# A four-layer graph network on one core: one product of the batch-norm shift in layer 0, half of layer 3's merged weights formed at the layer's end, pair sums added behind the next block

## The chip, the core and the metric

The kernel runs on one core of a Trainium2 chip. The core has five engines with instruction streams of their own: TensorE (PE, matrix products into PSUM), VectorE (DVE), ScalarE (ACT), GpSimd (POOL, here used for issuing transfers) and SyncE (SP, transfers only). Each engine takes its instructions in one fixed order and waits at an instruction until what it needs is there. The metric is the device time of one execution in microseconds; lower is better. Before the change it is 3288.74 us, the median of three runs (3287.61 to 3291.08).

## What is computed

Four graph layers on 2708 nodes with 512 features and a dense 0/1 adjacency matrix; after each layer comes `x = layernorm(x + layer(x))`. The change lies in layer 0, and touches weights of layer 3:

```python
# layer 0, X = x, n = 2708, H = 4 heads of D = 128; both patterns are adj
Xw = einsum('hnd,hde->hne', Xh, W)
f1 = einsum('hnd,hd->hn', Xw, V[:, 0, :, 0])
f2 = einsum('hnd,hd->hn', Xw, V[:, 1, :, 0])
sig = sigmoid(f1[:, :, None] + f2[:, None, :])
att = softmax over j of (adj * sig) where adj != 0, else 0
Xc  = concat over heads of att @ Xw
Xn  = batchnorm(Xc, enc_bn_gamma, enc_bn_beta)
emb = batchnorm(elu(Xn @ enc_mlp_W.T + enc_mlp_b) + Xn, ...)
Y   = elu(concat over heads of (att @ emb_h) @ W_h.T)
out = batchnorm(elu(Y @ dec_mlp_W.T + dec_mlp_b) + Y, ...)
# layer 1: A @ (x @ W + b) / column degree;  layer 2: softmax(e) with e = h @ h.T, h = x @ edge_w
# layer 3: softmax((x @ Wq + bq) @ (x @ Wk + bk).T / sqrt(512) + 2 adj) @ (x @ Wv + bv)
```

In layer 3 the kernel uses the merged matrix Wq @ Wk.T, of 512 x 512, in place of the two projections.

## The kernel before

Features are held transposed (four tiles of 128 features on the partitions, nodes along the free axis) or as rows (22 blocks of 128 nodes; the last has 20). Layer 0 makes two attention passes, the first over `xw` (values X W), the second over `emb`. Each runs over two halves of the target nodes (`hf`, 1354 columns) and, in each half, two pairs of heads (`p`); each such part goes over the 22 source blocks in a fixed order, `ORDER`. One block in the first pass:

- the adjacency block `a` comes from DRAM. With p = 0, DVE turns its zeros into a large negative number (L385 into `z`, L386 into `a`), and POOL writes it to `adj_d` for later parts. `z` has the tag "z", which has one buffer;
- ACT computes tanh for both heads into `t` (L396), DVE multiplies by the mask (L404), ACT takes the exponential in place (L405). Tiles `t` have the tag "t", with four buffers;
- PE multiplies the block's values with `t` into six PSUM banks `po` (L471, six products of 450 or 452 columns);
- PE adds up `t` over the rows into `psm` for the softmax's denominators (L494, eight small products). With p = 1, the blocks at places 4 to 19 are taken in pairs: DVE adds the odd block to the even one (L488), and PE sums once.

After 22 blocks `finish` copies `po` out (for the first pass `keep`, L580); the denominators go through DRAM, and the scaling and the batch-norm statistics (L608, L609) come during the next part.

The batch norm ahead of the encoder is folded into its weights: `enc_w` is scaled by `scale1` (L683 to L688), and the bias is the layer's bias plus the product of W with the norm's beta (in `keep`, after half 0 and p = 1, L583 to L586), minus the product of the scaled W with the mean (L732 to L742, within the encoder's first chunk). `small_product` takes four products of 1 x 512 (L546), a copy of the row on DVE (L549) and four products of 1 x 1 that turn the row into a column (L551). Its row in `keep` has the tag "z".

Between the passes PE transposes Wq and Wk (L668) into `wqT` and `wkT`, which lie in rows of `emb` that aren't filled yet, and forms the merged weights from them in four groups of four products (L696), which ACT scales and copies (L703) and POOL writes to `mqk_d` (L705). Then comes the query bias (`ps_u`), and the encoder (L724) in six chunks, whose result is transposed into `emb` (L756, L757).

At the end of layer 0 (`decode`, in the part that is final) PE runs the decoder's products (L859) chunk by chunk; `r_dec` takes buffers of the tag "t". The last chunk is followed by elu, statistics and the third batch norm on DVE and ACT. Layer 1 opens pools of its own over the memory of layer 0's: `hid_hi` and `hid_lo`, `raw`, `b1_sb`, `w1_sb`. Its first writes are a memset of a part of `hid_hi` and the copy `w1_sb` on DVE (L966, L976), both queued behind the norm's shift (`ready`), and the load of `b1_sb` (L102) on SP. It then scales the chunks (L983 on ACT), adds x (L990 on DVE), transposes and projects them (L996, L128 on PE).

A framework places all waits and fixes the order of each engine ahead of the run: by readiness in a plan of its own, and by program order among those that are ready. `issue_after(ins)` puts the instructions of its block behind `ins` on the same engine. Tiles with one tag share a given number of buffers.

## Time and profile before

| | us |
|---|---|
| median of three runs | 3288.74 |
| the profiled execution | 3290.97 |
| its span (first to last instruction) | 3289.2 |
| first attention pass, first product to last sum | 44.9 to 573.9 |
| merged weights to the last product of the encoder | 586.2 to 694.0 |
| second attention pass | 694.4 to 1145.0 |
| decoder's last product ends | 1201.6 |
| layer 1's first transposition | 1209.1 |

How to read the profile: PE, PEld (weight loads of PE), DVE, ACT, POOL and SP are the engines, SPq the queue of SP. Line numbers (L471) are those of the kernel before. In a timeline a line has the start, the time in us, the engine, the line, the operation, the tile written and the tile read, shapes and a count of instructions that were merged; in brackets stands how long the engine had been idle before, and what ended it. An fp32 product shows as two records, so "x12" of L471 are six products. The chain of waits is followed back from the last instruction, each time to what released it.

### The profile page before, as it was taken

How to read it: one execution, taken by the hardware profiler on the slowest of the kernel's cores; microseconds unless marked ns; L12 is line 12 of the kernel's file. 1: busy time of each engine (PE TensorE's matmuls, PEld its weight loads, DVE VectorE, ACT ScalarE, POOL GpSimd, SP SyncE). 2: the span in 40 equal slices, each digit the busy share in tenths (PEclk: the TensorE clock that was granted, in tenths of full speed). 3: DMA queues.
4: the chain of work that ended last, by engine and by line, in shares of the span. 5: the costliest groups of instructions: out<-in, count | busy, mean ns of one | idle time of the engine just before them, and what ended most of it. 6: DMA issues, size and time to landing. Idle time of an engine off the chain costs nothing.

```text
span 3289.2 us, 30359 instructions
## 1 busy us (share of the span) xinstructions
PE 3221.7 (98%) x10922; PEld 1722.4 (52%) x10922; DVE 1944.6 (59%) x3144; ACT 1348.5 (41%) x1512; POOL 129.7 (4%) x211
## 2 busy tenths in 40 slices
PE   8998999999999999999999999999999999999999
PEld 5443444454444445885555555554455555555554
DVE  7877977767687596445136666777252452543433
ACT  6887887557877753001133434443020120210211
POOL 1100100000000000000011000000000000000000
PEclk9999999999999999999999999999999999999999
DMA  8855863335555322550034444554211111111100
GB/s 283 305 187 171 302 233 124 106 102 183 185 179 172 134 81 67 144 145 21 0 102 133 122 124 136 148 159 125 68 49 33 44 31 43 40 34 43 36 24 20
DMA packets 172550, 381.45 MB, mean 116 GB/s; under 512 B 20938, under 2 KB 115094, under 8 KB 167982
## 3 DMA queue, kind: packets, MB, share of 16 engines
q1 hardware_dynamic: 156926, 308.16, 30.9%
q0 software_dynamic: 15472, 71.33, 5.8%
q8 instruction: 86, 1.41, 0.2%
q14 instruction: 66, 0.54, 0.1%
HBM read 307.22 MB, written 71.67 MB: 115 GB/s over the span
## 4 chain that ended last, share of the span: by engine, by line
PE 88%; DVE 5%; ACT 2%; DMA 2%; issue 1%; SPq 0%; DVEq 0%; ACTq 0%
PE po L1324 23%; PE po L471 19%; PE ps_s L1203 18%; PE ps_nb L1056 6%; PE ps_wide L1105 4%; PE psm L494 3%; DVE t L404 2%; PE ps_hid L128 2%; PE ps_sup L1501 2%; PE ps_o L1432 2%; PE ps_mlp L724 2%; PE ps_dec L859 2%; DMA a<-adj_d 1%; ACT t L405 1%; ACT t L396 1%
## 5 line engine op out<-in xcount | busy, mean ns | idle before, releaser
L404 DVE SCALAR_TENSOR_TENSOR t<-t,a 128x2708 f32<-128x2708 f32 (+1 forms) x156 | 462.2, 2975 | 124.1 <-ACT t L396 120.1
L396 ACT ACTIVATE t<-f1b,f2h 128x1354 f32<-128x1354 f32 (+1 forms) x312 | 428.3, 1413 | 60.5 <-PE po L471 28.7
L471 PE MATMUL po<-t,xw 128*128 128x452 f32 (+3 forms) x1056 | 415.9, 557 | 14.6 <-ACT t L405 14.6
L405 ACT ACTIVATE t<-t 128x2708 f32<-128x2708 f32 (+1 forms) x156 | 382.6, 2455 | 112.7 <-DVE t L404 112.4
L471 PE MATMUL po<-t,emb 128*128 128x452 f32 (+3 forms) x1056 | 403.1, 550 | 12.3 <-ACT t L405 9.2
L1203 PE MATMUL ps_s<-sup,hT 128*128 128x384 f32 (+1 forms) x1176 | 407.4, 490 | 0.0
L1324 PE MATMUL po<-sup,e 128*128 128x512 f32 x882 | 407.0, 595 | 0.0
L1324 PE MATMUL po<-e,xs 128*128 128x384 f32 (+1 forms) x1176 | 406.0, 489 | 0.0
L1635 DVE SCALAR_TENSOR_TENSOR e<-a_cols,ps_s 128x384 f32<-128x384 f32 (+1 forms) x154 | 85.5, 556 | 451.1 <-PE ps_s L1203 428.2
L471 PEld LDWEIGHTS po<-t,xw 128*128 128x128 f32 (+1 forms) x1056 | 191.5, 193 | 227.4 <-issue 202.0
L1203 PEld LDWEIGHTS ps_s<-sup,hT 128*128 128x128 f32 x1176 | 221.8, 190 | 164.2 <-issue 14.2
L471 PEld LDWEIGHTS po<-t,emb 128*128 128x128 f32 (+1 forms) x1056 | 194.9, 192 | 213.5 <-issue 188.7
L1324 PEld LDWEIGHTS po<-e,xs 128*128 128x128 f32 x1176 | 222.2, 190 | 160.2 <-issue 5.8
L1324 PEld LDWEIGHTS po<-sup,e 128*128 128x128 f32 x882 | 160.4, 190 | 159.3 <-issue 137.1
L1203 PE MATMUL ps_s<-hT 128*128 128x384 f32 (+5 forms) x672 | 211.1, 461 | 0.9 <-ACT sup L1508 0.7
L1302 ACT ACTIVATE e<-e 128x384 f32<-128x384 f32 (+1 forms) x308 | 151.7, 522 | 116.0 <-DVE e L1301 113.3
L1056 PE MATMUL ps_nb<-hid_hi,at 128*128 128x512 f32 x484 | 185.4, 390 | 0.4 <-DVE at L1048 0.4
L1550 ACT ACTIVATE a_cols<-a_cols,neg_big 128x384 f32<-128x384 f32 (+1 forms) x154 | 94.7, 617 | 220.9 <-DMA a_cols<-in_adjT_dram 183.3
L1056 PE MATMUL ps_nb<-hid_lo,at 128*128 128x512 f32 x462 | 179.9, 389 | 0.0
L108 ACT ACTIVATE ln_rstd<-ln_rstd 128x1 f32<-128x1 f32 (+1 forms) x88 | 17.2, 201 | 391.7 <-DVE ln_rstd L107 391.2
L1301 DVE TENSOR_TENSOR e<-e,nmax 128x384 f32<-128x384 f32 (+1 forms) x308 | 163.1, 552 | 23.3 <-ACT nmax L1294 23.3
L1203 PEld LDWEIGHTS ps_s<-hT 128*128 128x128 f32 x672 | 123.1, 190 | 89.5 <-issue 19.4
(252 smaller groups left out, 3325.8 us busy)
## 6 DMA issues: line engine op xcount, KB each, us to landing
a<-adj_d SPq DMA_DIRECT2D x110, 677.0 KB
a_cols<-in_adjT_dram SPq DMA_DIRECT2D x378, 192.0 KB
a<-in_adjT_dram SPq DMA_DIRECT2D x42, 677.0 KB
adj_d<-a POOLq DMA_DIRECT2D x42, 677.0 KB, 5.5
raw<-in_adjT_dram SPq DMA_DIRECT2D x105, 256.0 KB
kept<-t POOLq DMA_DIRECT2D x16, 1354.0 KB, 6.8
t<-kept SPq DMA_DIRECT2D x16, 1354.0 KB
a_cols<-in_adjT_dram SPq DMA_DIRECT2D x63, 202.0 KB
```

Of the source, the lines that this page charges most:

```text
L396: nc.scalar.activation(tv[:, k, :], f1b[:n, k, :w], AF.Tanh, bias=f2h[:n, jt, h : h + 1], scale=0.5,)
L404: step = nc.vector.scalar_tensor_tensor(tv, tv, GUARD, ab, ALU.add, ALU.mult)
L405: nc.scalar.activation(tv, tv, AF.Exp, scale=0.5)
L471: nc.tensor.matmul(po[HB * k + q][:, :qw], values[r : r + n, jt, h * P : (h + 1) * P], t[r : r + n, k, q0 : q0 + qw], start=(place == 0), ...
L494: nc.tensor.matmul(sums[k][32 * r : 32 * r + 32, :SW], ones32[:m], whole[:m, k, q0 + qw - SW : q0 + qw], start=(place == 0), stop=(place = ...
L1056: nc.tensor.matmul(pos[it][:n], at, half[:, jt, :], start=(jt == 0 and k == 0), stop=(jt == NT - 1),)
L1105: nc.tensor.matmul(ps[:, :width], w(c, o), xt(c), start=(c == 0), stop=(c == C - 1),)
L1203: nc.tensor.matmul(ps[:, b * P : w], keys[:, c, j0 : j0 + P], st["q"][:, c, b * P :], start=(c == 0), stop=(c == C - 1),)
L1301: nc.vector.tensor_tensor(e, e, st["nmax"][:, :w], ALU.add)
L1302: nc.scalar.activation(e, e, AF.Exp)
L1324: nc.tensor.matmul(out, lhsT, rhs, start=(k == 0), stop=(k == NT - 1))
L1550: nc.scalar.activation(a, a, AF.Identity, bias=neg_big[: a.shape[0]], scale=1.0e30)
```

## The change

Five things are done.

1. The bias of the encoder is formed at once: `shift1` (beta minus mean times scale) is computed after the batch norm's scale, and one small product of it with the unscaled `enc_w` gives the bias. The product in `keep` and the one in the encoder's first chunk are gone. `enc_w` is scaled after the product.
2. Of the four groups of the merged weights, group 0 stays ahead of the shift's product and group 1 comes behind it. POOL writes `wkT` and half of `wqT` to DRAM (`wkT_d`, `wqT_d`), and each quarter of `mqk_d` gets its first half.
3. The other two groups are formed at the end of `decode`: `wkT_d` and `wqT_d` are loaded into two buffers of the tag "t", PE forms the groups behind the decoder's last product (`last_dec`) in two of the `po` banks, ACT copies them into the second half of one of the buffers, and POOL writes them to `mqk_d`.
4. In the paired blocks of the first pass, the add on DVE is issued behind the multiplication (L404) of the next block, and the pair's sums come just ahead of the next block's products in the program.
5. The row of the product in `keep`, with the tag "z", is gone with it.

```diff
--- before.py
+++ after.py
@@ -1,3 +1,4 @@
+from functools import partial
 from contextlib import ExitStack, nullcontext
 import concourse.bass as bass
@@ -163,6 +164,9 @@
     dram = ctx.enter_context(tc.tile_pool(name="dram", bufs=1, space=bass.MemoryType.DRAM))
     adj_d = dram.tile([N, N], F32, name="adj_d")
     mqk_d = dram.tile([C, P, C, P], F32, name="mqk_d")
+    wqT_d = dram.tile([P, C, C // 2 * P], F32, name="wqT_d")
+    wkT_d = dram.tile([P, C, F], F32, name="wkT_d")
     qscale = float(1.0 / F**0.5)
     uq = const.tile([P, C], F32, name="uq")
@@ -428,7 +432,7 @@
                     sums = None
                     if first and rest is None:
                         sums = sum_tiles()
-                    before = None
+                    before = waiting = None
                     for place, jt in enumerate(ORDER):
                         n = BLOCKS[jt][1]
@@ -464,6 +468,9 @@
                                 for q in range(HB)
                             ]
                             po = [both[q][:, k, :] for k in range(HP) for q in range(HB)]
+                        if waiting is not None:
+                            waiting(step)
+                            waiting = None
                         for k in range(HP):
                             h = HP * p + k
                             for q, (q0, qw) in enumerate(HCH[hf]):
@@ -478,26 +485,37 @@
                         if not first:
                             continue
-                        if prepare or not ALONE <= place < NT - LAST:
-                            whole, m = t, n
-                        elif place % 2 == 0:
+                        single = prepare or not ALONE <= place < NT - LAST
+                        if not single and place % 2 == 0:
                             before = t
                             continue
+                        def add_up(whole, m, more, first_one, last_one, behind=None):
+                            if more is not None:
+                                with tc.issue_after(behind.ins):
+                                    nc.vector.tensor_tensor(
+                                        whole[: more.shape[0], :, :w],
+                                        whole[: more.shape[0], :, :w],
+                                        more,
+                                        ALU.add,
+                                    )
+                            for k in range(HP):
+                                for r, (q0, qw) in enumerate(SCH[hf]):
+                                    nc.tensor.matmul(
+                                        sums[k][32 * r : 32 * r + 32, :SW],
+                                        ones32[:m],
+                                        whole[:m, k, q0 + qw - SW : q0 + qw],
+                                        start=first_one,
+                                        stop=last_one,
+                                    )
+                        if single:
+                            add_up(t, n, None, place == 0, place == NT - 1)
                         else:
-                            whole, m = before, P
-                            nc.vector.tensor_tensor(
-                                whole[:n, :, :w], whole[:n, :, :w], tv, ALU.add
-                            )
-                        for k in range(HP):
-                            for r, (q0, qw) in enumerate(SCH[hf]):
-                                nc.tensor.matmul(
-                                    sums[k][32 * r : 32 * r + 32, :SW],
-                                    ones32[:m],
-                                    whole[:m, k, q0 + qw - SW : q0 + qw],
-                                    start=(place == 0),
-                                    stop=(place == NT - 1),
-                                )
+                            waiting = partial(add_up, before, P, tv, False, False)
                     later += finish(hf, p, po, sums if first else rb) or []
             for work in later:
                 work()
@@ -580,10 +598,6 @@
                         taken[q % 2] = copy(
                             ft[:, HP * p + k, h0 + q0 : h0 + q0 + qw], po[HB * k + q][:, :qw]
                         )
-                if hf == 0 and p == 1:
-                    row = att.tile([P, HW], F32, tag="z", name="row", bufs=1)[:1, :F]
-                    ps = small_product(po[0], mlp_w[0], prm_sb[:, B_ENC, :], row)
-                    nc.vector.tensor_tensor(bias[:, 0, :], ps, prm_sb[:, MB_ENC, :], ALU.add)
                 sm = [att.tile([P, BW], F32, tag="rs", name="sm") for _ in range(HP)]
                 if not final:
                     for k in range(HP):
@@ -640,6 +654,7 @@
             attention_pass(xw, True, att, psum, keep, f1b, blocks, spread, rest, taken)
             scale1, mean1 = batch_scale(stats, G_ENC, "bn1")
+            shift1 = batch_shift(scale1, mean1, B_ENC, "bn1")
             emb = rows_tile("emb")
@@ -676,21 +691,9 @@
             tc.tile_pool(name="ps_c", bufs=1, space=PSUM) as psum,
         ):
-            (enc_w,) = mlp_w
-            for c in range(C):
-                if c % 2:
-                    nc.scalar.activation(
-                        enc_w[:, c, :], enc_w[:, c, :], AF.Copy, scale=scale1[:, c : c + 1]
-                    )
-                else:
-                    nc.vector.tensor_scalar(
-                        enc_w[:, c, :], enc_w[:, c, :], scale1[:, c : c + 1], None, ALU.mult
-                    )
-            stats = stats_tile("stats_b", NCH)
             mqk = emb[:, NT - 3 * C : NT - 2 * C, :]
-            for c in range(C):
+            def merged(c):
                 ps = psum.tile([P, F], F32, tag="misc", name="ps_m", bufs=2)
                 for o in range(C):
                     nc.tensor.matmul(
@@ -701,10 +704,38 @@
                         stop=(o == C - 1),
                     )
                 nc.scalar.activation(mqk[:, c, :], ps, AF.Copy, scale=qscale)
+            merged(0)
+            (enc_w,) = mlp_w
+            row = emb[:1, NT - 3 * C - 2 : NT - 3 * C, :]
+            pm = small_product(
+                psum.tile([P, F], F32, tag="misc", name="ps_shift", bufs=2),
+                enc_w,
+                shift1,
+                row[:, 1, :],
+            )
+            nc.vector.tensor_tensor(bias[:, 0, :], pm, prm_sb[:, MB_ENC, :], ALU.add)
+            nc.vector.tensor_scalar(bias[:, 1, :], bias[:, 0, :], 1.0, None, ALU.subtract)
+            for c in range(C):
+                if c % 2:
+                    nc.scalar.activation(
+                        enc_w[:, c, :], enc_w[:, c, :], AF.Copy, scale=scale1[:, c : c + 1]
+                    )
+                else:
+                    nc.vector.tensor_scalar(
+                        enc_w[:, c, :], enc_w[:, c, :], scale1[:, c : c + 1], None, ALU.mult
+                    )
+            stats = stats_tile("stats_b", NCH)
+            nc.gpsimd.dma_start(wkT_d, wkT)
+            nc.gpsimd.dma_start(wqT_d, wqT[:, :, half * P :])
+            merged(1)
             for o in range(C):
-                nc.gpsimd.dma_start(mqk_d[o], mqk[:, :, o * P : (o + 1) * P])
-            row = emb[:1, NT - 3 * C - 2 : NT - 3 * C, :]
+                nc.gpsimd.dma_start(
+                    mqk_d[o][:, :half, :], mqk[:, :half, o * P : (o + 1) * P]
+                )
             pu = small_product(
                 psum.tile([P, F], F32, tag="misc", name="ps_u", bufs=2),
                 wkT,
@@ -729,17 +760,6 @@
                             stop=(c == C - 1),
                         )
                     pss.append(ps)
-                    if ci == 0 and o == 0:
-                        pm = small_product(
-                            psum.tile([P, F], F32, tag="misc", name="ps_mean", bufs=2),
-                            enc_w,
-                            mean1,
-                            row[:, 1, :],
-                        )
-                        nc.vector.tensor_tensor(bias[:, 0, :], bias[:, 0, :], pm, ALU.subtract)
-                        nc.vector.tensor_scalar(
-                            bias[:, 1, :], bias[:, 0, :], 1.0, None, ALU.subtract
-                        )
                 for o in range(C):
                     dst = ft[:, o, c0 : c0 + w]
                     r = elu(
@@ -768,6 +788,7 @@
             dec_w = load_mlp(dec_wT, "dec_w")
             links = {}
             spare = []
+            last_dec = [None]
             def centre(pm):
@@ -856,7 +877,7 @@
                     q0, qw = HCH[hf][q]
                     ps = psum.tile([P, BANK], F32, tag="misc", name="ps_dec", bufs=2)
                     for c in range(C):
-                        nc.tensor.matmul(
+                        last_dec[0] = nc.tensor.matmul(
                             ps[:, :qw],
                             dec_w[:, c, o * P : (o + 1) * P],
                             t[:, c, q0 : q0 + qw],
@@ -942,6 +963,38 @@
                     if q == 0:
                         centre(po[0])
                     mlp(q, 3, st, True)
+                rest = [
+                    att.tile([P, HP, HW], F32, tag="t", name=name, bufs=4).rearrange(
+                        "p k w -> p (k w)"
+                    )
+                    for name in ("wk_again", "wq_again")
+                ]
+                wk_again = rest[0][:, : C * F].rearrange("p (c o) -> p c o", c=C)
+                wq_again, mqk = [
+                    rest[1][:, k * half * F : (k + 1) * half * F] for k in range(2)
+                ]
+                wq_again = wq_again.rearrange("p (c o) -> p c o", c=C)
+                mqk = mqk.rearrange("p (c o) -> p c o", c=half)
+                nc.sync.dma_start(wk_again, wkT_d)
+                nc.sync.dma_start(wq_again, wqT_d)
+                with tc.issue_after(last_dec[0].ins):
+                    for c in range(half):
+                        for o in range(C):
+                            nc.tensor.matmul(
+                                po[1 + c],
+                                wq_again[:, o, c * P : (c + 1) * P],
+                                wk_again[:, o, :],
+                                start=(o == 0),
+                                stop=(o == C - 1),
+                            )
+                for c in range(half):
+                    nc.scalar.activation(mqk[:, c, :], po[1 + c], AF.Copy, scale=qscale)
+                    nc.gpsimd.dma_start(
+                        mqk_d[:, :, half + c, :].rearrange("o p i -> p o i"),
+                        mqk[:, c, :].rearrange("p (o i) -> p o i", o=C),
+                    )
             attention_pass(emb, False, att, psum, decode)
         dsum = small.tile([P, NT], F32, tag="dsum", name="dsum")
```

## The prediction, made before the changed kernel was run

> **What bounds the kernel now.** I read the page first: busy times, then the chain that ended last.
>
> ```profile
> PE 3221.7 (98%) x10922; PEld 1722.4 (52%) x10922; DVE 1944.6 (59%) x3144; ACT 1348.5 (41%) x1512; POOL 129.7 (4%) x211
> PE 88%; DVE 5%; ACT 2%; DMA 2%; issue 1%; SPq 0%; DVEq 0%; ACTq 0%
> ```
>
> TensorE (PE) is busy 98% of the span and holds 88% of the chain. So time is won in two ways: PE work that moves into a gap of PE, and gaps of PE that close. All that is changed lies before 1210 us, and I looked for the gaps there in the timelines. The passes of the first attention are called (half, pair) = (0,0), (0,1), (1,0), (1,1).
>
> The largest gap is at the seam from (0,1) to (1,0). PE, then VectorE (DVE), in order of time:
>
> ```profile
> 299.32 1.35 PE L494 MATMUL psm<-t,ones 128*32 128x340 f32 x16
> 300.49 3.59 PE L546 MATMUL po<-enc_w,prm_sb 128*1 128x512 f32 x8
> 304.86 1.05 PE L551 MATMUL po<-ones,row 1*128 1x1 f32 x8 [0.77 <-DVE row L549]
> 314.14 6.29 PE L471 MATMUL po<-t,xw 128*128 128x452 f32 x12 [8.24 <-ACT t L405]
> ```
> ```profile
> 285.79 2.97 DVE L404 SCALAR_TENSOR_TENSOR t<-t,a 128x2708 f32<-128x2708 f32 x1
> 297.91 1.16 DVE L580 COPY ft<-po 128x452 f32<-128x452 f32 x2 [9.15 <-PE po L471]
> ...
> 305.94 0.16 DVE L586 TENSOR_TENSOR enc_bias<-po,prm_sb 128x4 f32<-128x4 f32 x1 [1.14 <-PE po L551]
> 306.02 0.87 DVE L385 TENSOR_SCALAR z<-a 128x1354 f32<-128x1354 f32 x1
> ```
>
> PE runs the small product of the shift, then waits 8.24 us for the next pass's first exponential. DVE had idled 9.15 us before the copies, yet prepared the next block (L385) only at 306.02. The reason is a buffer: `row` of the small product has tag z with one buffer, and so has `z` of L385. At the seam (1,0) to (1,1), where no product stands, PE shows no gap at all (sums at 445.60, next attention product at 446.89).
>
> The second place is the paired sums, where the add must wait until PE has read what it overwrites, and the next block's multiplication stands behind it on DVE:
>
> ```profile
> 267.98 2.98 DVE L488 TENSOR_TENSOR t<-t 128x2708 f32<-128x2708 f32 x1 [4.33 <-PE po L471]
> 270.87 5.86 DVE L404 SCALAR_TENSOR_TENSOR t<-t,a 128x2708 f32<-128x2708 f32 x2
> ```
> ```profile
> 272.35 1.35 PE L494 MATMUL psm<-t,ones 128*32 128x340 f32 x16
> 276.39 10.94 PE L471 MATMUL po<-t,xw 128*128 128x452 f32 x24 [2.69 <-ACT t L405]
> ```
>
> The third and fourth are the merged weights, in PE's full row at 586, and the gap before layer 1, to which half of them goes:
>
> ```profile
> 586.20 13.97 PE L696 MATMUL ps_m<-emb 128*128 128x512 f32 x32 [0.91 <-DVE ft L638]
> ```
> ```profile
> 1184.79 16.79 PE L859 MATMUL ps_dec<-ot,dec_w 128*128 128x452 f32 x44
> 1209.11 0.48 PE L996 MATMUL tp_out<-ident,ot 128*128 128x128 f32 x1 [7.53 <-DVE ot L990]
> ```
>
> **A, the small product at 300 goes.** PE's work ends there at 299.32+1.35 = 300.67. Without `row`, DVE is free from 288.76. Tanh of the next pass's first two blocks is done by 290 and 295 (ScalarE, ACT, rows of L396 at 287.37 and 292.36). L385 0.87, L386 1.57 and L404 2.97 then end at about 294, and the exponential of 2.46 at about 298, before 300.67. Block 1 follows at about 302, needed at 306.7. In the steady state DVE takes 5.98 us a block (316.97 to 322.95) and PE 6.03, so the lead holds. PE starts 13.47 us earlier. The first block also took 6.29 instead of 4.82: the granted clock is 0.50 in 314.1 to 317.1 and 0.99 after. With no idle time before it, 1.47 goes too: **-14.9**. Bounds: all of it; or, if DVE's first preparation stays behind the copies (which end at 301.4), L385, L386, L404 and the exponential give 309.1, so -5.0. I take the first, since the seam at 445 has the same copies and no gap.
>
> **B, pair sums behind the next block.** DVE's order becomes next L404, then add; PE's sums come later. At the place quoted, tanh of the next block is done near 268.2 (263.19 and 266.87, 1.4 each), so L404 ends at 271.1, the exponential at 273.6, and PE, free of attention products at 272.35, waits 1.25 instead of 2.69. The sums wait for the add (271.1+2.98 = 274.1) and fit in behind. Gain 1.44, once in (0,1) and once in (1,1) (2.69 again at 549.78): **-2.9**. The clock loss after the gap (10.94 for 9.37) I leave: a gap of 1.41 at 238.23 has one too. The gap at 238.23 stays, since the add there already stands behind the next L404 and is late through its own 2.97. Best bound: idle and slow time of both passes' second halves (7.8 and 8.5, of which 3.1 each stay) gives -10. Worst bound: the even block's buffer is held until the later sums, in a ring of four; a delay of 0.7 for each of 16 pairs is +11. With -14.9 from A, this is the least sure term.
>
> **C, stage at 586.** Removed from this place: two of four merged products, 13.97/2 = 6.99. Small products there remain two (shift and query bias for query bias and mean): 3.59+1.05 each. The shift is ready at 587.95 plus two small DVE instructions of 0.2, before the first merged product ends (589.69). Scaling enc_w now waits for that product (to 593.3), 0.9 on DVE and 1.3 on ACT, needed by the first encoder product near 601: hidden behind the second merged product and the query bias; uncovered it would cost 1.3. The bias comes near 600 instead of 619.82, so the 0.73 us that PE waits at 624.26 goes. Added on POOL: two writes of 1.5 MB together, and four halves; at 0.76 to 1.05 an issue, on a queue that is idle from 580 to 603. They compete with the loads for the second attention, whose first four blocks are ready by 619 and needed at 694. **-7.7**, bounds -5.6 (two waits as at 304.86 and 607.53) to -9.1.
>
> **D, the moved half at the end.** The reload stands on SP's queue between 1152 and 1204.70, where it is empty. Its buffers (tag t) are free at 1159.8 and 1175.6, and 1.5 MB at the 370 to 397 GB/s of that stretch takes 4 us: there by 1181, 20 us early. PE does the products from 1201.58 to 1208.57, inside its gap. But layer 1's buffers lie where this pool's lay, and the trace shows that their first use waits for the whole pool:
>
> ```profile
> SPq L102 <- DVE ot L883: 52.2, 1, 52.2
> ```
>
> This is layer 1's first load (`b1_sb`), held until 1204.70 by the last reader of `r_dec`. Its bytes were an `a` buffer, whose last reader (L404) ended at 1134.99. So after the change, layer 1's first writers wait for the last use of the new tiles: the POOL write of mqk. On DVE that is the memset L966 (1206.96), and behind it stand `w1_sb` and every L990 that PE waits for. Products end 1208.57, ACT copy +0.28+0.58 = 1209.43, issue +0.30, landing
>
> ```profile
> DMA to landing us min/median/max: 3.5/4.4/6.0
> ```
>
> so 1213.2, 1214.1 or 1215.7. I take 3.5, as nothing else moves then: 1213.2-1206.96 = **+6.3**. Bounds: +8.8; and, if only bytes count, layer 1 starts as before and PE, idle for 0.5 us instead of 7.5, skips its slow start (first block's products 6.26 for 3.60): -2.7. The two ACT copies (0.58) hide in the same wait, even if the second goes ahead of the root at 1205.89.
>
> The Trainium skill (DMA: Bandwidth & Descriptors, section Anatomy of one DMA — SWDGE (gpsimd) path) prices such a transfer at 2.0 us plus bytes over 436 GB/s, most of it the wait for the write's receipt, which a late wait hides and an immediate one does not. By that estimate 256 KB lands in 2.6 us, D is +5.4 and the time 0.9 lower; it speaks against putting a write right before a wait. This trace's shortest is 3.5.
>
> Sum: -14.9-2.9-7.7+6.3 = **-19.2**, on a span of 3289.2: 3270.0. The profiled run took 3290.97, 1.8 more than its span and 2.2 more than the median; from the median, 3288.74-19.2 = **3269.5**.
>
> **Rivals.**
> R1, layer 1 isn't held: D = -2.7, time 3260.5. For: the byte map puts the reload buffers in what hid_lo takes. Against: the wait of 52.2 us above.
> R2, the seam closes only in part: A = -5.0, time 3279.4. For: DVE's order is fixed ahead, and the copies stood before L385. Against: the seam at 445.
> R3, slower: the paired sums make PE wait, with the sums ahead of the next attention products in PE's order while the add stands behind a whole L404. A+C+D = -16.3 over 16 pairs: it decides from 1.0 us a pair; at the full 2.97 of an add, +47.5-16.3 gives 3319.9. For: ring of four, odd buffers held by the `kept` writes. Against: PE needs 10.99 us a pair and ACT some 10.4, so the add has room.
> R4, given back: the time won at the seam is lost again in (1,0), because DVE (5.98) and the transfers (0.82 share) have hardly room under PE's 6.03. A = 0, time 3284.4: no change.
>
> **How the numbers follow.** Runs before spread by 0.1%; a difference under 0.2% (6.6 us) I count as none. Chances: forecast 0.55 (own range 3263 to 3276), R1 0.13, R2 0.12, R3 0.10, R4 0.10. Range 3257 to 3284 holds the forecast, R1 and R2. Faster 0.79 (the first three, less the edge of R2), same 0.11, slower 0.10.
>
> **What would show it.** A: no L546 near 300 and no PE gap between L494 and L471 there; L385 before the copies. B: the gap of 2.69 near 276 and 549 shrinks, L488 behind the next L404. C: half of 13.97 at 586, the second attention's first product some 25 us earlier than 694.42. D: PE busy for 7 us after the last decoder product, then idle some 7 us again, DVE's memset waiting for mqk_d's write. Wrong if (1,0) shows new gaps, or if PE's L494 waits on L488 in most pairs.

## The result, and the profile after

The changed kernel takes 3268.4 us (median of 4 runs, 3268.23 to 3272.62), the kernel before 3288.89 on the same chip: a ratio of 0.9941, 95% interval 0.9930 to 0.9953. On a second chip it was 3269.34 against 3288.72, again 0.9941 (0.9929 to 0.9953). That is 19.4 to 20.5 us faster; forecast were 19.2 us and 3269.5.

The page of the changed kernel, busy times and the chain that ended last:

```profile
PE 3212.9 (98%) x10906; PEld 1717.4 (53%) x10906; DVE 1944.1 (59%) x3144; ACT 1346.8 (41%) x1512; POOL 132.9 (4%) x215
PE 87%; DVE 6%; ACT 3%; DMA 2%; issue 1%; SPq 0%; DVEq 0%; ACTq 0%
```

PE's busy time fell by 8.8 us (sixteen instructions fewer, and fewer of the rest at a low clock), the span by 18.4 in the profiled executions (3289.2 to 3270.8). The rest came out of PE's gaps. Five marks on PE cut the span into stages that can be compared between kernels (us, profiled executions):

| kernel | F | M | S | L | R | median, ratio to before on the same chip |
|---|---|---|---|---|---|---|
| before | 336.10 | 120.09 | 507.16 | 33.73 | 2053.89 | |
| changed | 318.74 | 113.46 | 507.29 | 37.56 | 2055.77 | 3268.4, 0.9941 |
| changed, second chip | 318.82 | 113.18 | 504.46 | 37.45 | 2055.29 | 3269.34, 0.9941 |
| seam alone | 322.95 | 127.96 | 504.06 | 33.11 | 2053.91 | 3278.48, 0.9975 |
| pair sums alone | 331.62 | 120.41 | 504.82 | 33.56 | 2053.61 | 3282.61, 0.9989 |
| merged half alone | 336.33 | 112.81 | 502.95 | 38.26 | 2054.00 | 3282.54, 0.9986 |
| changed, pair sums undone | 319.77 | 113.36 | 507.33 | 39.14 | 2054.51 | 3270.86, 0.9954 |
| changed, `z` held | 326.42 | 113.01 | 504.52 | 38.34 | 2053.46 | 3275.55, 0.9960 |
| changed, product | 318.22 | 115.21 | 505.61 | 37.49 | 2054.28 | 3271.59, 0.9949 |
| changed, other source | 318.36 | 113.42 | 503.89 | 32.88 | 2054.17 | 3265.9, 0.9932 |
| changed, jobs at even places | 318.15 | 113.51 | 503.93 | 38.25 | 2055.04 | 3268.98, 0.9939 |
| changed, held weights | 318.12 | 113.28 | 504.67 | 33.21 | 2053.98 | 3264.14, 0.9929 |
| changed, tanh behind | 315.76 | 112.99 | 504.90 | 37.52 | 2055.54 | 3267.99, 0.9937 |
| changed, both | 315.82 | 115.42 | 504.27 | 33.26 | 2054.49 | 3263.29, 0.9922 |

The kernel before was timed beside each of them and took 3286.35 to 3289.08, so medians of different rows are compared by their ratios. F runs from the paired sums' wait near 238 us (1.41 or 1.42 us in every run) to the first transposition of Wq (L668 before); M from there to the second attention's first product; S to the end of the decoder's last product; L to the transposition of layer 1's seventh block; R to the end. Nothing was changed in R, and in S only the two reloads on SP's queue came in: S and R scatter by some 4 and 2 us between executions, S by 2.8 for the same kernel, so a whole time says less about a part than its stage does. F has scatter of its own: no edit touches the wait near 238 or a like one near 511 in (1,1), but the sums behind each took 1.35 us in some executions and up to 2.49 in others, and the stretch as far as the wait near 276 (or 549) was up to 1 us longer by that. A and B of the prediction fall into F, C into M, D into L.

Changed against before: F -17.36, M -6.63 and L +3.83, together -20.16, and +2.01 in S and R.

**The seam** (answers to the lines at 299 to 314 and 285 to 306 before). PE in order of time, then DVE:

```profile
297.28 1.35 PE L507 MATMUL psm<-t,ones 128*32 128x340 f32 x16
298.56 1.78 PE L478 MATMUL po<-t,xw 128*128 128x452 f32 x4
```
```profile
279.69 0.86 DVE L389 TENSOR_SCALAR z<-a 128x1354 f32<-128x1354 f32 x1
...
297.29 2.23 DVE L598 COPY ft<-po 128x452 f32<-128x452 f32 x4
```

The sums end at 298.63 and the next pass's product starts at once; the wait of 8.24 is gone, and so is the slow first block. DVE prepares that block 18 us ahead of the copies.

**The pass (1,0) then has a wait that it did not have.** PE:

```profile
363.58 1.35 PE L507 MATMUL psm<-t,ones 128*32 128x340 f32 x16
364.87 1.79 PE L478 MATMUL po<-t,xw 20*128 20x452 f32 x12
366.58 1.34 PE L507 MATMUL psm<-t,ones 20*32 20x340 f32 x16
370.20 7.14 PE L478 MATMUL po<-t,xw 128*128 128x452 f32 x12 [2.27 <-ACT t L409]
```

Behind the short block of 20 rows PE waits 2.27 us, and the block after it takes 7.14 instead of 4.82. Before, that place (384.92) had no wait and took 6.51. Counted from the wait near 238, PE came to the short block 16.80 us earlier than before; from there to the wait near 511 it took 2.03 longer.

**The pair sums** (answers to 267.98 to 276.39). DVE, then PE:

```profile
268.06 2.98 DVE L408 SCALAR_TENSOR_TENSOR t<-t,a 128x2708 f32<-128x2708 f32 x1 [4.66 <-ACT t L400]
270.96 2.97 DVE L498 TENSOR_TENSOR t<-t 128x2708 f32<-128x2708 f32 x1
273.84 5.93 DVE L408 SCALAR_TENSOR_TENSOR t<-t,a 128x2708 f32<-128x2708 f32 x2
```
```profile
273.59 1.02 PE L478 MATMUL po<-t,xw 128*128 128x452 f32 x2 [1.42 <-ACT t L409]
274.54 1.35 PE L507 MATMUL psm<-t,ones 128*32 128x340 f32 x16
275.82 4.06 PE L478 MATMUL po<-t,xw 128*128 128x452 f32 x10
280.48 1.78 PE L478 MATMUL po<-t,xw 128*128 128x452 f32 x4 [0.60 <-ACT t L409]
```

The multiplication now stands ahead of the add, and the wait of 2.69 became 1.42 (forecast: 1.25). But the add now delays the multiplication after it, whose exponential comes 0.60 late: 0.67 of idle time is won in each pass, not 1.44. The low clock behind the wait is gone too.

**The stage of the merged weights** (answers to the full row at 586.20):

```profile
568.58 3.67 PE L699 MATMUL ps_m<-emb 128*128 128x512 f32 x8 [0.91 <-DVE ft L652]
572.18 3.59 PE L564 MATMUL ps_shift<-enc_w,bn_shift 128*1 128x512 f32 x8
575.71 1.98 PE L699 MATMUL ps_m<-emb 128*128 128x512 f32 x4
578.41 1.05 PE L569 MATMUL ps_shift<-ones,emb 1*128 1x1 f32 x8 [0.72 <-DVE emb L567]
579.39 1.98 PE L699 MATMUL ps_m<-emb 128*128 128x512 f32 x4
```

Two groups, 7.63 us, instead of 13.97, with the shift's product between them. Its row is 0.72 late.

**Layer 1's start** (answers to 1184.79 to 1209.11). PE, POOL and DVE in order of time; from the table of waits the line of SP's queue (us in all, times, longest); and from the view of L994, POOL's late writes, their time from issue to landing:

```profile
1177.31 7.03 PE L985 MATMUL po<-wk_again,wq_again 128*128 128x512 f32 x16
1186.09 1.10 PE L1049 MATMUL tp_out<-ident,ot 128*128 128x128 f32 x8 [1.75 <-ACT wq_again L993]
1191.08 8.62 PE L129 MATMUL ps_hid<-w_sb,ot 128*128 128x512 f32 x16 [3.90 <-DVE ln_rstd L110]
```
```profile
1186.32 0.77 POOL L994 DMA_DIRECT2D mqk_d<-wq_again  x1 [3.70 <-ACT wq_again L993]
```
```profile
1183.62 2.59 DVE L1043 TENSOR_TENSOR ot<-ot,xs 128x452 f32<-128x452 f32 x4 [0.83 <-ACT ot L1036]
1186.85 1.30 DVE L115 BATCH_NORM_STATS2 ln_st<-tp_out 128x6 f32<-128x512 f32 x2 [0.64 <-PE tp_out L1049]
...
1188.81 0.60 DVE L1043 TENSOR_TENSOR ot<-ot,xs 128x452 f32<-128x452 f32 x1
1189.46 0.48 DVE L1019 MEMSET hid_hi<- 128x512 f32 x1
1189.87 1.17 DVE L1029 COPY w_sb<-xs 128x2048 f32<-128x2048 f32 x1
```
```profile
SPq L103 <- DMA mqk_d<-wq_again: 34.1, 2, 29.7
```
```profile
DMA to landing us min/median/max: 2.7/2.7/2.7
```

The second write of `mqk_d` is issued at 1186.32 and lands 2.7 us later, at 1189.0. The memset of `hid_hi` starts at 1189.46, the copy `w1_sb` behind it ends at 1191.04, and only then the projection starts (the bracket names L110, which ends at the same time as the copy; on the second chip the same wait of 3.90 is put down to the copy, L1029). The load of `b1_sb` (L103) was held by the writes, as SP's row shows. For the memset no row shows that: DVE works without a pause from 1186.85 to 1189.41, on statistics and adds that stand ahead of the memset in its order, so the landing came 0.4 us before the memset's turn. The adds of L1043 ran from 1183.62, ahead of the memset, so that two blocks were transposed before PE's wait.

### The profile page after: what moved, and what is told of

It reads as the page before. It is cut to its first block, busy times and chain, and to the rows that moved or that the text cites. A ratio compares the mean times of both kernels' runs of the same rounds, so it can differ in the third digit from the quotient of the medians.

```text
span 3270.8 us, 30357 instructions
## 1 busy us (share of the span) xinstructions
PE 3212.9 (98%) x10906; PEld 1717.4 (53%) x10906; DVE 1944.1 (59%) x3144; ACT 1346.8 (41%) x1512; POOL 132.9 (4%) x215
## 3 DMA queue, kind: packets, MB, share of 16 engines
q8 instruction: 86, 1.41, 0.2%
## 4 chain that ended last, share of the span: by engine, by line
PE 87%; DVE 6%; ACT 3%; DMA 2%; issue 1%; SPq 0%; DVEq 0%; ACTq 0%
PE po L1377 23%; PE po L478 18%; PE ps_s L1256 17%; PE ps_nb L1109 7%; PE ps_wide L1158 4%; PE psm L507 3%; DVE t L408 2%; PE ps_hid L129 2%; PE ps_sup L1554 2%; PE ps_o L1485 2%; PE ps_dec L880 2%; ACT t L400 2%; ACT t L409 1%; PE ps_mlp L755 1%; DMA a<-adj_d 1%
```

## The experiments

**Each part alone.** First the seam: no product in `keep`, and the shift's product at the encoder.

```diff
-                if hf == 0 and p == 1:
-                    row = att.tile([P, HW], F32, tag="z", name="row", bufs=1)[:1, :F]
-                    ps = small_product(po[0], mlp_w[0], prm_sb[:, B_ENC, :], row)
...
             (enc_w,) = mlp_w
+            pm = small_product(psum.tile(...), enc_w, shift1, row[:, 1, :])
             for c in range(C):
```

> The kernel before with the seam part alone: no small product and no tile `row` at about 300 us; the shift's small product stands ahead of the scaling of enc_w at about 586, and the product of the mean is gone. Pair sums and merged weights as before. My theory (the seam's 8.24 us gap is the buffer of tag z, and the block after it then runs at the full clock): the first attention product of the pass (1,0) starts 13 to 16 us earlier, 2 to 3 us are given back inside that pass, and the whole is 11 to 14 us faster than before (the lost wait at 624 included). R2 (the seam closes only in part): 5 to 6 us faster, and a gap of about 8 us before the first product of (1,0). R4 (all given back, since DVE and the transfers have no room): under 3 us faster, with gaps in (1,0) that sum to some 12 us.

3278.48 us, ratio 0.9975 (0.9967 to 0.9984): 7.9 faster, below what I expected, and the table says where. F is shorter by 13.15, as expected (0.85 of it lies ahead of the seam, behind the untouched wait near 238), with the gap in (1,0) at its place (2.28). A second wait stands in (1,0), which the changed kernel does not have:

```profile
337.40 4.82 PE L471 MATMUL po<-t,xw 128*128 128x452 f32 x12 [1.26 <-ACT t L405]
```

ACT's tanh (at 332.25) had waited 2.27 us for a buffer `t` that was still being written to `kept` (its releaser is `DMA kept<-t`). M is longer by 7.87. PE there:

```profile
575.43 6.12 PE L546 MATMUL ps_shift<-enc_w,bn_shift 128*1 128x512 f32 x8 [3.32 <-DVE bn_shift L540]
603.83 1.33 PE L551 MATMUL ps_u<-ones,emb 1*128 1x1 f32 x8 [1.93 <-DVE emb L549]
605.09 13.94 PE L729 MATMUL ps_mlp<-ft,enc_w 128*128 128x452 f32 x28
```

This kernel has no group of merged weights ahead of the shift's product, so PE waits 3.32 us for the shift (the wait that stood there before was 0.91) and then works at a low clock (6.12 for 3.59). In the changed kernel group 0 covers that wait: C's "hidden" rests on it. That is 4.9 of the 7.87. Most of the rest lies behind the query bias's row: PE waits 1.93 for it (1.36 before) and then works 8 us at a mean clock of 0.57. One execution does not tell whether that belongs to the edit or to chance.

Then the pair sums alone (`add_up` and its place, as in the change; the rest as before).

> The kernel before with the pair sums alone moved behind the next block; the small product at the seam and the merged weights as before. My theory (half a wait of 2.69 us goes in each of two passes, and in (1,1) some of PE's slow time behind it): 3 to 5 us faster, the wait before the attention product near 276 and 549 down from 2.69 to about 1.4. R3 (PE waits for the sums or for the ring of four buffers): slower by some us. A third reading, that it is worth something only beside the other parts: within 1 us of before.

3282.61 us, 0.9989 (0.9980 to 0.9998): 3.7 faster; F -4.48, M and L as before within 0.4. Of the 4.48, 0.97 lies behind the wait near 511, which the edit leaves at 1.41 (the sums took 2.47 there before and 1.35 here), so 3.5 is the part's own. My theory holds in direction and size.

Then the merged half alone (groups 2 and 3 at the end, `mqk_d` written in two halves; both small products as before).

> The kernel before with half of the merged weights alone moved to the end; the mean's small product stays behind the first encoder product. My theory: the stage at 586 is shorter by half of the 13.97 us row, about 7; layer 1 starts later by what its first writers are held, 3.8 us as in the changed kernel; in sum 2.5 to 4 us faster than before. If layer 1 were not held: 7 or more faster. If the hold is longer without the other parts: down to no difference.

3282.54 us, 0.9986 (0.9977 to 0.9995): 3.8 faster; M -7.28, L +4.53. The whole agrees with the forecast; the hold at layer 1 is there without the other parts.

The three gains in time add up to 15.4 us, 4 to 5 short of the change. The M of the first run has the size of the difference: without it, the differences of F, M and L in the three runs add up to -20.6, in the change itself to -20.2. So the parts aren't independent: without a group of merged weights ahead of it, the shift's product waits (4.9 us with the low clock); the rest of that M is not explained.

**The pair sums taken out of the change** (add at once, sums behind the pair, as before).

> The changed kernel with the pair sums put back (add at once, sums right behind the pair). If the parts simply add up: slower than the changed kernel by 3 to 5.3 us, that is 15 to 17.5 us faster than before. If the pair sums only matter because DVE's order around the earlier pass (1,0) changed with them: either the pass (1,0) loses its new gap of 2.27 us at 370, and the difference is under 2 us, or the gap stays.

3270.86 us, 0.9954 (0.9942 to 0.9967). By the medians it is 15.5 us faster than before, 4 to 5 less than the changed kernel, as if the parts added up. The gap at 370 stays (2.27 at 371.70), so it doesn't come from the pair sums. In the profiled execution F is only 1.03 longer than in the changed kernel, against 4.48 between the two kernels without the seam part. That 1.03 is itself a mixture: the sums near 238 took 1.35 instead of 2.16, and PE waits 1.40 more at 336.23, the second wait of the seam run again (with both parts in place, that wait is 0.42 at most). PE of this run:

```profile
275.78 9.37 PE L475 MATMUL po<-t,xw 128*128 128x452 f32 x24 [2.69 <-ACT t L409]
```

The wait is 2.69 as before, but the 24 instructions behind it took 9.37 (10.94 in the kernel before). The price of such a wait depends on the clock that PE is granted behind it. So this part is worth 1.3 us of idle time (two times 0.67) and up to 3.0 us of clock (10.94 and, at 549.78, 10.78 in the kernel before, against 9.37).

**What made the wait at the seam: the buffer or the product?** The tile of tag z is put back, with a DVE copy and without a product:

```diff
+                if hf == 0 and p == 1:
+                    row = att.tile([P, HW], F32, tag="z", name="row", bufs=1)[:1, :F]
+                    nc.vector.tensor_copy(row[:, :BW], po[0][:1, :BW])
                 sm = [att.tile([P, BW], F32, tag="rs", name="sm") for _ in range(HP)]
```

> The changed kernel, with the tile `row` (tag z, one buffer) back at the seam before (1,0), written only by one DVE copy out of the attention's PSUM, which nothing reads; no product on PE. My theory (the buffer of tag z kept DVE from preparing the next pass's first block, not PE's product): the preparation falls behind the copies of the pass that ends, PE waits again before the first product of (1,0), by 7 to 10 us, and the end of (1,0) comes 6 to 9 us later than in the changed kernel (its gap at 370 of 2.27 then goes). The rival (PE's product and its clock made the gap): no wait at the seam, under 2 us of difference.

3275.55 us, 0.9960 (0.9945 to 0.9975). DVE, and PE at the seam:

```profile
296.88 0.61 DVE L603 COPY row<-po 1x452 f32<-1x452 f32 x1
297.42 1.14 DVE L598 COPY ft<-po 128x450 f32<-128x450 f32 x2
298.49 0.91 DVE L608 TENSOR_SCALAR sm<-psm 128x340 f32<-128x340 f32 x2
299.32 0.85 DVE L389 TENSOR_SCALAR z<-a 128x1354 f32<-128x1354 f32 x1
```
```profile
307.40 1.88 PE L478 MATMUL po<-t,xw 128*128 128x452 f32 x2 [8.84 <-ACT t L409]
```

One copy of 0.61 us brings the whole wait back: L389 stands behind the user of the buffer, and F is 7.68 longer (0.97 of it behind the untouched wait near 511, whose sums took 2.05 for 1.35). The gap at 370 is gone in this run. So the tile in that tag suffices for the wait, without the product. (The same copy into a tile of another tag was not run; the copy by itself takes 0.61 us.) The product's own time, 3.59+1.05 and the wait of 0.77 between them, is about the rest of A. The product without the tile:

```diff
+                if hf == 0 and p == 1:
+                    for c in range(C):
+                        nc.tensor.matmul(po[0][:1, :F], prm_sb[:, B_ENC, c : c + 1], mlp_w[0][:, c, :], ...)
```

> The changed kernel, with the four products 1x512 of the former small product back on PE at the seam, into the attention's PSUM, which nothing reads; no tile of tag z. My theory: PE needs 3.59 us more there, the preparation stays ahead, no wait of 8 us; up to 3.6 us slower than the changed kernel, less what the gap of 2.27 at 370 gives back (so 1 to 4). The rival (the product made the gap): 10 to 15 us slower.

3271.59 us, 0.9949 (0.9932 to 0.9965); F 318.22. There is no wait at the seam, but PE's order has the product within the next pass's first block (at 300.56), so this run does not test it at the old place. It costs nothing in F all the same: its 3.59 us are repaid by the gap at 370, which is gone. M is 1.75 longer, because the shift's row came 2.44 us late; in the ten executions that have that row between two groups it came 0.18 to 2.44 late, so this isn't put down to the edit.

**What ends the wait at layer 1?** The two late writes take their data from a constant, so no tile of the closed pool has a DMA as its last reader. Nothing ties the writes to the layer's end any more, and they were issued at 1.5 and 2.4 us, at the kernel's start:

```diff
                         mqk_d[:, :, half + c, :].rearrange("o p i -> p o i"),
-                        mqk[:, c, :].rearrange("p (o i) -> p o i", o=C),
+                        ones.unsqueeze(1).to_broadcast([P, C, P]),
```

> The changed kernel, with POOL's two late writes of mqk_d taken from the constant tile `ones` in place of the attention's buffer, so that the second half of layer 3's merged weights is other data; ScalarE's copies stay. My theory (layer 1's first writers wait for the last reader of the closed pool's tiles, the two writes' landing): they are released by ScalarE's second copy at about 1186 instead of the landing at 1189, the memset of the hidden layer starts about 3 us earlier, and the projection of layer 1's first block 2.5 to 3.5 us earlier. R1's reading (the memory in question is not shared, the wait is for something else): the memset starts as in the changed kernel, within 0.5 us. Another (SP's or POOL's queue is late, not the pool): no change either.

3265.9 us, 0.9932 (0.9917 to 0.9947). DVE and PE:

```profile
1185.75 0.48 DVE L1019 MEMSET hid_hi<- 128x512 f32 x1
...
1187.23 1.28 DVE L115 BATCH_NORM_STATS2 ln_st<-tp_out 128x6 f32<-128x512 f32 x2
```
```profile
1187.37 7.13 PE L129 MATMUL ps_hid<-w_sb,ot 128*128 128x512 f32 x16 [0.71 <-DVE w_sb L1029]
```

Counted from the decoder's last product (1176.95 here, 1177.47 in the changed kernel) the memset starts 8.80 us later instead of 11.99, right behind ACT's second copy, and L is 4.68 shorter. So the late writes make the hold, and R1 falls. How they hold the memset is shown less well. In this run it also stands in another place of DVE's order, ahead of the statistics (L115) that it stood behind. SP's load waits for the landing by its own row; for the memset the wait for the landing and the order that was fixed ahead of the run come to the same time within 0.4 us, and no run separates them.

**What makes the gap in (1,0)?** My first theory was DVE, which has 5.97 us of work a block against PE's 6.03 there.

```diff
-                        if place > (3 if first else 0) and later:
+                        if place > (3 if first else 0) and later and not (first and place % 2):
```

> The changed kernel, with the scaled jobs of the pass before taken on DVE only at every other place of the first attention. My theory (in (1,0) DVE needs 5.97 us a block with those jobs, against PE's 6.03, so the lead of the first product is not regained before the short block of 20 rows, and PE waits 2.27 us behind it): that wait goes or is under 0.5, and the whole is 2 to 4 us faster than the changed kernel. If ScalarE's exponentials or the loads set the wait: the gap stays at about 2.3 and the time is the same within 1 us. If the jobs then pile up behind the pass: slower.

3268.98 us, 0.9939 (0.9924 to 0.9954), and at 370.00 the gap of 2.28 stands unchanged, though DVE had the block that PE needs ready 0.81 us after the start of the short block, 1.30 in the changed kernel. That theory fell. What is left shows on ACT, in the changed kernel and in the run with the product:

```profile
365.06 2.74 ACT L400 ACTIVATE t<-f1b,f2h 128x1354 f32<-128x1354 f32 x2 [0.94 <-PE psm L507]
367.71 2.44 ACT L409 ACTIVATE t<-t 128x2708 f32<-128x2708 f32 x1
```
```profile
362.98 2.74 ACT L400 ACTIVATE t<-f1b,f2h 128x1354 f32<-128x1354 f32 x2 [0.43 <-PE psm L507]
365.65 2.46 ACT L409 ACTIVATE t<-t 128x2708 f32<-128x2708 f32 x1
```

In the changed kernel (first fence) DVE had finished the block that PE needs at 366.17. Its exponential stands on ACT behind a tanh pair of a later block, which waits for PE's sums to free one of the four buffers `t`, and both take 5.2 us. A full block on PE covers that (6.03), the short one does not (1.79+1.34). In the run with the product (second fence) the tanh pair ahead of the same exponential belongs to one block less far ahead. The sums that it waits for come a full block of PE earlier (361.56, where the last ones before the short block are at 367.58), and the exponential is done at 368.11, 3.75 before PE asks for it at 371.86. Both orders were fixed when the kernels were built. So I forced the second order:

```diff
+                second = first and hf > 0 and p == 0 and len(exps) > 1
+                with tc.issue_after(exps[-2].ins) if second else nullcontext():
+                    for k in range(HP):
...
-                nc.scalar.activation(tv, tv, AF.Exp, scale=0.5)
+                exps.append(nc.scalar.activation(tv, tv, AF.Exp, scale=0.5))
```

> The changed kernel, with ScalarE's tanh of each block of the pass (1,0) put behind the exponential of the block two before it, in ScalarE's order; nothing else. My theory (there ScalarE has one tanh pair more ahead of the exponentials than in the run with the product at the seam; that pair waits for a buffer of the ring of four, which PE's sums free, and the exponential that PE needs next stands behind it): the gap of 2.27 at 370 goes, and most of the slow products behind it (7.14 for 4.82); the end of (1,0) comes 3 to 4.6 us earlier. If the ring itself is the limit and not the order: the gap stays within 0.5 of 2.27. If the lead of the tanh is needed elsewhere: new gaps in (1,0), and no gain.

3267.99 us, 0.9937 (0.9925 to 0.9950); F 315.76, that is 3.06 less than the changed kernel on the same chip. Of this, 0.96 lies ahead of the short block, behind the untouched wait near 238 (sums of 1.35 for 1.99); 2.1 is the edit's, less than the 3 to 4.6 that I expected. ACT and PE:

```profile
365.74 2.46 ACT L411 ACTIVATE t<-t 128x2708 f32<-128x2708 f32 x1 [0.47 <-DVE t L410]
```
```profile
368.26 6.51 PE L481 MATMUL po<-t,xw 128*128 128x452 f32 x12 [0.79 <-ACT t L411]
```

The gap shrinks to 0.79, and what ACT waits for now is DVE. So ACT's order was the cause of 1.5 of 2.28 us (of 1.3 in the run with both edits below, where 0.96 is left); in what is left ACT waits for DVE. In the whole time the gain (1.35 between medians) can't be told from scatter.

**Layer 1 without the hold on its weights, and both together.** The first two blocks are projected from `w1_held`, which lies outside the closed pool:

```diff
-            for ci in range(len(early), NCH):
-                load_x(x_held, ci)
...
+                if ci == 1:
+                    for late in range(len(early), NCH):
+                        load_x(x_held, late)
...
-                    project_rows(ps, ot[:, :, i0 : i0 + n], w1_sb, n)
+                    project_rows(ps, ot[:, :, i0 : i0 + n], w1_held if it < 2 else w1_sb, n)
```

> The changed kernel, with layer 1's first two blocks projected from `w1_held` (which the held copy `w1_sb` is made from) and the last chunk of layer 1's input, which takes the buffer of `w1_held`, loaded after the first chunk's adds instead of before. My theory (PE waits 3.90 for the copy behind the held memset, and only for that): the first projection starts right behind the transpositions, block 2's transposition comes some 17.5 us after the last decoder product instead of 22.07, and the whole is 3 to 4.5 us faster than the changed kernel. If the held memset then stops the chain somewhere else (the first writes of hid_hi): under 1.5 us faster. If the late load of the last chunk is late: slower.

3264.14 us, 0.9929 (0.9915 to 0.9942). PE, then DVE:

```profile
1182.72 0.66 PE L1050 MATMUL tp_out<-ident,ot 128*128 128x128 f32 x4 [1.74 <-ACT wq_again L993]
1183.22 3.60 PE L129 MATMUL ps_hid<-xs,ot 128*128 128x512 f32 x8
```
```profile
1189.98 0.75 DVE L1059 SCALAR_TENSOR_TENSOR full<-ps_hid,ln_rstd,b_sb 128x512 f32<-128x512 f32 x1 [1.67 <-DMA b_sb<-in_b_dram]
```

The projection starts right behind the transposition and runs at the full clock (3.60 a block). Block 2, the third, is transposed 16.41 us after the decoder's last product (1174.11 to 1190.52), 22.07 in the changed kernel. Then the load of `b1_sb`, held by the same writes, is late (1.67 on DVE), and PE loses 1.09 of it at 1199.52. L is 4.24 shorter than in the changed kernel on this chip.

> The two edits together (first two blocks from `w1_held`; tanh of (1,0) behind the exponential two before). They lie 800 us apart and I expect them to add: 6 to 9 us faster than the changed kernel, 25 to 29 faster than before. If what the first one gains is waited away at layer 1 or later: as the better of the two alone.

3263.29 us, 0.9922 (0.9909 to 0.9936): 25.4 faster than before and 6.05 faster than the changed kernel on the same chip, at the lower edge of what I expected. The stages carry both gains (F -3.00, L -4.19), less 2.24 in M, where the row of the shift came 1.01 late and PE's clock fell. The range of its runs (3260.60 to 3264.31) lies below all runs of the changed kernel (from 3265.89).

The unchanged control:

> The changed kernel as it is, on the same chip as the next three, so that their differences can be taken on one chip: 18 to 21 us faster than before.

It was 19.4 us faster; the first time it was 20.5.

## Why the prediction was right

The sum held: -19.2 forecast, -18.4 in the profiled executions (-20.2 in the three stages that the change touches) and -19.4 and -20.5 in the medians. Each of its four terms was off, by 0.6 to 2.6 us and with both signs, so part of the agreement is that these cancel, which is luck.

**A, -14.9 forecast, -12.3 to -12.9 measured** (F of the seam part: -13.15 alone, of which 0.85 lies ahead of the seam; -12.88 on top of the pair sums). The cause of the wait is shown: the tile of tag z. The step that failed is "In the steady state DVE takes 5.98 us a block (316.97 to 322.95) and PE 6.03, so the lead holds." I weighed DVE against PE over full blocks only. The lead has to cover the short block too, where PE needs 3.1 us, and ACT's order, which I had not looked at, lets it fall behind a tanh pair: 2.27 us of wait and a slow block. The prediction had named new gaps in (1,0) as a sign of being wrong, and one came.

**B, -2.9 forecast.** The mechanism is right, the term mis-sized both ways. The idle time won is 0.67 per pass instead of 1.44: "PE, free of attention products at 272.35, waits 1.25 instead of 2.69" was right within 0.2 (1.42), but I did not ask for whom the moved add is late next. The clock loss that I "leave" did go in this execution. So some -3.5 by the run alone, and by its idle time -1.3 where the clock holds anyway.

**C, -7.7 forecast, -6.63 measured.** Half of the merged products went as counted (13.97 to 7.63). The wait of 0.73 at 624 that I let go returned as three others: 0.72 for the shift's row, and 0.48 and 0.98 where `tp_emb` waits in the encoder. Against that the query bias's row, 1.36 late before, came in time.

**D, +6.3 forecast, +3.8 measured.** The hold by the late writes is shown, and its length was right: the memset starts 11.99 us after the decoder's last product instead of 5.38, which is 6.6 later. (That the landing itself released it is shown for SP's load only.) Wrong was "behind it stand `w1_sb` and every L990 that PE waits for". The adds were placed ahead of the memset in DVE's order, and PE transposed two blocks during the hold; only the projection waited. Two smaller errors cancel: the write landed after 2.7 us, not 3.5, while ACT's second copy came 0.7 later than I had it, behind four L1036. The Trainium skill's fit (DMA: Bandwidth & Descriptors, section Anatomy of one DMA — SWDGE (gpsimd) path) gives an estimate of 2.6 us for 256 KB; the 2.7 of the trace agrees with it, and the row that I took in its place, from the four writes of `mqk_d` near 600, was the poorer guide.

**The rivals.** R1 fell by SP's wait for the late writes and by the other-source run. R2 did not occur: no wait is left at the seam. R3 did not occur: PE waits for an add at two places in F, 1.41 us each, where before there were three (1.41, 0.88, 1.41). R4 came true for some 2 us, not for the whole, and mostly not for its reason: ACT's order made 1.5 of the 2.27. The transfers that R4 also names show in the second wait of the seam run.

## What to carry to other kernels

When a wait goes, follow the lead that it gave to the engines behind it, up to the shortest block of the next pass, and on every engine in the loop: here ACT's order took back what DVE's and PE's averages said was safe. A one-buffer tag that is shared by a rare small tile and by the loop's own tile orders the whole loop behind the small one. Work moved to the end of a pool holds the first users of the next pool until its last reader is done, and a DMA write as the last reader adds its landing, as SP's row shows; what the next stage needs first is best kept outside that pool, as the run with the held weights shows. And a clock that varies behind untouched waits can pass for the effect of an edit: compare such places too before a stage's difference is put down to it.

## What the runs showed of the hardware

The same wait costs PE different clocks. Behind the wait of 2.69 us near 276 the 3 us that follow look like this in the kernel before, in the seam part alone, and in the change without pair sums (stretch, its length, PE's busy time and instructions, mean granted clock, DMA share, GB/s):

```profile
276.40:279.40 3.00, 3.00 (x4) 0.50 0.75 253
```
```profile
275.40:278.40 3.00, 3.00 (x6) 0.73 0.72 233
```
```profile
275.80:278.80 3.00, 3.00 (x8) 1.00 0.73 258
```

The mean clock was 0.50, 0.73 or 1.00, and PE did four, six or eight instructions, under much the same load of the DMA engines (0.72 to 0.75). Even the 1.41 us wait at 238 was followed by a sum of 1.35 us in some executions and of up to 2.49 in others. The Trainium skill (TensorE: Matmul & The Clock Gate, Part 1: The HAM clock gate) has the clock follow a window that runs freely, so that the loss varies from run to run; the loss in the three lines above varies too, but no line shows the window. For a reader of such profiles it means that closing a gap of 1 to 3 us is worth its length and, by chance, up to about as much again (behind the 2.27 us at 370, 7.14 for 4.82).
